# The top of layer 0 in a four-layer kernel: weights of layer 2 in four transfers, transpositions between the first products, small folds by row products

## The chip, the core and the metric

The kernel runs on one core of a Trainium2 chip. Everything is computed in fp32. The metric is device time in microseconds (us) from the first to the last instruction of one execution; the time of a kernel is the median of its runs.

The engines run side by side, each with its own instruction stream: TensorE (PE: products, and PEld: the loading of their stationary operand), VectorE (DVE), ScalarE (ACT), GpSimd (POOL) and SyncE (SP), which here only issues transfers. ScalarE and GpSimd issue transfers too. "ACTq" or "SPq" in a profile is the issue of a transfer on that engine's stream, "L776" is line 776 of the kernel.

## The reference

Four layers follow each other on an input x of 2 x 512 x 32 x 32. The change touches the top of layer 0, where two unrelated things are computed: the first steps of layer 0's attention, and products of weights that layer 2 needs much later. Layer 0, cut to what is spoken of here:

```python
xn = _bn(x, bn1_g, bn1_b)
q = _gconv1x1(xn, qw)                       # 8 groups of 64 channels
qg = q.reshape(b * GROUPS, DH, H, W)
off = conv(qg, off_dw_w, stride 4, 6 x 6, per channel)      # 36 taps
off = gelu(off + off_dw_b)
off = tanh(einsum('bchw,oc->bohw', off, off_pw_w)) * OFF_SCALE
...
pos = grid_q[:, :, None, :] - grid_kv[:, None, :, :]
bias = sign(pos) * log1p(abs(pos))
bias = relu(bias @ cpb_w1 + cpb_b1)
bias = relu(bias @ cpb_w2 + cpb_b2)
bias = (bias @ cpb_w3 + cpb_b3)
sim = einsum('bhid,bhjd->bhij', qh, kh) + bias
...
```

Layer 2:

```python
qkv = einsum('oc,bchw->bohw', w_qkv, xn) + b_qkv
attn = softmax(einsum('bci,bcj->bij', q, k) * scale)
out = einsum('bcj,bij->bci', v, attn)
proj = einsum('oc,bchw->bohw', w_proj, out) + b_proj
```

Its weights can be multiplied with each other ahead of time: Wq with Wk, and Wv with W_proj (the two "folds", 512 x 512 each), and the biases likewise (two vectors of 512: Wk times the bias of q, and W_proj times the bias of v, plus b_proj).

## The kernel before

`layer0` begins with loads and a stretch of preparation, and then runs a loop over `i` (256 iterations) that makes layer 0's attention bias: in each iteration VectorE forms four table sums (`first`, L599: 128 x 1024 sums of two short tables), TensorE multiplies them by `cpb_w2` in four parts (`second`, L616, tile z: 32 output partitions for each of four points, so that four products stand in different quarters of the partitions), ScalarE applies the relu (L625), and VectorE joins two parts (`joined`, L630). `first` runs up to 7 sums ahead of the products. Its results stand in a ring of eleven tiles: three of their own, then six pieces of the tile that holds layer 2's `qkv2` weights, and two of `proj2`'s; so a sum can be written there only when these weights are no longer read, and the sum number 11 needs the tile of number 0, which all four parts of the first iteration read.

The order on every engine is fixed: `in_order` makes each instruction follow the one before it in the program's text on the same engine. What one engine waits for thus holds up all that stands behind it on that engine. Pieces of work are written as generators, and calls of `advance` and `drain` lay out by hand how they interleave:

- `offsets(t)`: the query product pq (L389), its copy with bias `qb` to `qpad` by ScalarE (L391), 36 taps (for t = 0 on VectorE, L423 and L425), Gelu, the small product po (L441), tanh (`th`), a change of ScalarE's function table, sign, abs and log (`sgn`, `pos`), and the store of the tables `slog_d`. `load_tabs` and `scale_tab` bring them back for `first`.
- `bias_weights`: sorts and turns `cpb_w2`: prow, below, pcount, pw2t, pparts, pw2, and many small VectorE operations on the tile `few`.
- `key_weights`: transposes the block-diagonal `qw` and `kw` (twq, L789, with ScalarE's copies qwn and kwn, L791) and multiplies them (pkw, L797; copy kq_w, L798). Its result is first used in the loop.
- `transposed(j, k)`: the four 128 x 128 transpositions of chunk k of Wq, Wk or Wv (tile tw, L776) and two ScalarE copies of 128 x 256 to `nat` (tile bridge, L778), twelve times.
- `fold`: eight products over four chunks (tile pf, L135), every second one followed by a ScalarE copy of 128 x 1024 (`folded`, L835) and a store. The folds 4 to 7 read `proj2` in place.
- `small_fold`: the bias of q spread over the partitions by four products with the identity (row, L843), four products and sums with it on VectorE (`t2_b`, L849 and L850), and, in four steps, four products of one column each with `proj2` (pb, by `accumulate`, L135), then `o2_b` on VectorE (L855).

Products and transpositions write to three rotating PSUM tiles (`zt`); the tile `sim` is a fourth. The pool `h2q` has three buffers, which take the relu results of parts 1 and 3 in the loop and short-lived rows before it.

The loads: SP issues the constants, `qw`, `kw` (two transfers each, L229), `cpb_w2`, `vb2` and chunks 1 to 3 of x[0] (L242); ScalarE issues chunk 0 of x[0] (L218), then `qkv2_w` in four transfers and `proj2_w` in four (`load_w`, L119). GpSimd first clears `qw`, `kw` and `vw` whole (L224). `late_loads` (x[1] and `vw`) and the loop's tables follow on SP. In the loop the generators `small_steps` (what is left of it), `offsets(1)` and `samples(0)` are chained as `behind`, two steps for each iteration.

Of the kernel before, what the change touches and what calls it, by code (L numbers as in the profile page):

```python
# [19 lines left out]
P = 128  # L20
B, C, H, W = 2, 512, 32, 32
HW = H * W
CC = C // P
# [56 lines left out]
def kernel(ctx: ExitStack, tc: tile.TileContext, a: dict, out: bass.AP):  # L80
# [111 lines left out]
    def layer0(l0, fold_d, t2_b, o2_b):  # L192
# [26 lines left out]
        qkv2, proj2 = load_w(wa, "wa", [a["qkv2_w"], a["proj2_w"]], nc.scalar)  # L219
# [3 lines left out]
        for w in bd.values():  # L223
            nc.gpsimd.memset(w, 0.0)  # L224
# [7 lines left out]
        load_groups("kw")  # L232
# [9 lines left out]
        nc.sync.dma_start(out=xs[0][:, 1:, :], in_=a["x"][0, P:, :].rearrange("(k p) n -> p k n", p=P))  # L242
# [16 lines left out]
        pqb = zt([P, NPAIR], "pqb")  # L259
        for pr in range(NPAIR):  # L260
            nc.tensor.matmul(pqb[:, pr : pr + 1], bd["qw"][:, pr, :], col("bn1_b", pr), start=True, stop=True)
        nc.vector.tensor_copy(qb, pqb)
# [509 lines left out]
        def transposed(j, k):  # L772
# [4 lines left out]
            for i in range(2):  # L777
                nc.scalar.copy(nat[j][i][:, :, k * P : (k + 1) * P], tw[:, 2 * i : 2 * i + 2, :])  # L778
# [20 lines left out]

        steps = offsets(0)  # L800
        advance(steps, 2)
        bias_steps = bias_weights()
        next(bias_steps)
        key_steps = key_weights()
        advance(key_steps)
        advance(steps, 4)
        advance(bias_steps)
        advance(steps, 20)
        drain(key_steps)
# [6 lines left out]
        nat = [[next(h2p).rearrange("p (k n) -> p k n", k=2) for _ in range(2)] for _ in range(3)]  # L816
        wq, wk, wv = [lambda o, n, w=w: w[o // 2][:, o % 2, n] for w in nat]
        everything = slice(0, C)
        pb2 = ps_s.tile([P, CC], F32, name="pb2", tag="sim")
# [19 lines left out]
        def small_fold():  # L839

            row = zt([P, C], "row")
            for o in range(CC):
                nc.tensor.matmul(  # L843
                    row[:, o * P : (o + 1) * P], col("qkv2_b", o).to_broadcast([P, P]), ident, start=True, stop=True
                )
            yield
# [4 lines left out]
            for m in range(CC):  # L851
                n = slice(m * P, (m + 1) * P)
                accumulate(pb2[:, m : m + 1], [(proj2[:, o, n], vb2[:, o : o + 1]) for o in range(CC)])
                yield
            nc.vector.tensor_tensor(o2_b, pb2, col("proj2_b", 0, CC), ALU.add)  # L855

        fold_steps, small_steps = fold(), small_fold()
        for k in range(CC):
# [8 lines left out]
        advance(small_steps)  # L867
        advance(fold_steps)
        advance(small_steps)
# [3 lines left out]
        for _ in range(5):  # L873
            advance(fold_steps)
            advance(small_steps)
        drain(fold_steps)

# [1388 lines left out]
```

## Time and profile before

| | |
|---|---|
| median of 3 runs | 3350.77 us (3349.29 to 3352.3) |
| the profiled execution: its own time | 3353.46 us |
| the profiled execution: span | 3351.7 us, mean granted TensorE clock 0.998 |
| VectorE, ScalarE, GpSimd busy | 80%, 54%, 20% of the span |
| first product of the loop (z, L616) | 59.64 us |
| HBM read, written | 71.46 MB, 10.83 MB |

A profile shows one execution. Busy time is counted for each engine; the chain of waits goes back from the last instruction, at each step to what released it, and names its pieces with start and length; the timeline lists the instructions of an engine with, in brackets, the idle time before them and what ended it. The page divides the span into 40 slices of 84 us, so the whole preparation lies in the first one.

### The profile page before, as it was taken

The page shows a single profiled execution, that of the slowest core. Times are in us where ns is not written, and L with a number is a line of the kernel's source. Part 1 is how long each engine was busy: PE and PEld are TensorE (multiplying, and loading weights), DVE is VectorE, ACT ScalarE, POOL GpSimd, SP SyncE. Part 2 cuts the span into 40 slices and gives each one's busy share as a digit, 9 for nine tenths or more (in the row PEclk, how much of TensorE's full clock was granted, in tenths as well). Part 3 has the DMA queues.
Part 4 walks back from the last instruction along what each step waited for, and adds up shares of the span by engine and source line. Part 5 has one row for each costly group of instructions (what it writes and reads, how often), then busy time and mean ns, then how long its engine had stood idle before and what let it go on. Part 6 is the DMA issues. An engine that isn't in the chain of part 4 may idle for free.

```text
span 3351.7 us, 61808 instructions
## 1 busy us (share of the span) xinstructions
PE 3323.8 (99%) x24813; PEld 1611.7 (48%) x24813; DVE 2673.0 (80%) x3540; ACT 1805.5 (54%) x2774; POOL 676.7 (20%) x804
## 2 busy tenths in 40 slices
PE   9999999999999999999999999999999999999999
PEld 4333333332333332333333339999953443687777
DVE  6999999999999799999999976455446465665556
ACT  4866877877877577877877652122136245122221
POOL 0333333333333233333333310000000000000000
PEclk9999999999999999999999999999999999999999
DMA  5778787787787577787787751000100000000111
GB/s 166 157 161 166 153 168 156 152 166 153 158 167 155 103 162 155 159 169 152 158 166 157 161 135 58 14 8 14 52 0 14 26 29 20 7 7 3 30 32 36
DMA packets 142488, 343.97 MB, mean 103 GB/s; under 512 B 36464, under 2 KB 51440, under 8 KB 141424
## 3 DMA queue, kind: packets, MB, share of 16 engines
q0 software_dynamic: 68400, 231.26, 36.5%
q1 hardware_dynamic: 72496, 103.95, 10.7%
q8 instruction: 197, 3.23, 0.4%
q10 hardware_dynamic: 1296, 4.72, 0.4%
q14 instruction: 99, 0.81, 0.1%
HBM read 71.46 MB, written 10.83 MB: 25 GB/s over the span
## 4 chain that ended last, share of the span: by engine, by line
PE 82%; DVE 9%; issue 5%; DMA 2%; ACT 1%; POOL 1%; DVEq 0%; SPq 0%; POOLq 0%; ACTq 0%
PE z L616 38%; PE pma L135 6%; PE pw L1435 6%; PE pmb L135 5%; PE pmv L1435 4%; PE score L1614 3%; PE pv L1626 3%; DVE wa L599 3%; PE pm L1435 3%; PE score L1435 3%; PE pmt L1435 1%; PE ppr L1435 1%; DVE h L599 1%; DMA bridge<-h 1%; DVE bridge L630 1%
## 5 line engine op out<-in xcount | busy, mean ns | idle before, releaser
L616 PE MATMUL z<-wa,cpb_w 128*32 128x512 f32 x11904 | 1779.2, 593 | 5.8 <-ACT h L625 3.7
L625 ACT ACTIVATE h<-z,b2h 128x1024 f32<-128x1024 f32 x768 | 851.3, 1114 | 347.9 <-PE z L616 310.6
L616 PE MATMUL z<-h,cpb_w 128*32 128x512 f32 x4480 | 983.2, 593 | 1.6 <-ACT h L625 1.6
L616 PEld LDWEIGHTS z<-wa,cpb_w 128*32 128x32 f32 x11904 | 497.2, 110 | 888.2 <-issue 778.1
L599 DVE CUSTOM_DVE_ANT_1 wa<-tab,tab 128x1024 f32<-128x1024 f32 x744 | 878.1, 1216 | 1.3 <-PE z L616 1.1
L616 PEld LDWEIGHTS z<-h,cpb_w 128*32 128x32 f32 x4480 | 256.6, 110 | 328.6 <-issue 292.1
L599 DVE CUSTOM_DVE_ANT_1 h<-tab,tab 128x1024 f32<-128x1024 f32 x280 | 332.9, 1216 | 2.3 <-PE z L616 2.2
L630 DVE SCALAR_TENSOR_TENSOR h<-h,turn,h 128x1024 f32<-128x1024 f32 x256 | 326.8, 1276 | 4.3 <-ACT h L625 4.3
L625 ACT ACTIVATE bridge<-z,b2h 128x1024 f32<-128x1024 f32 x162 | 180.8, 1116 | 121.4 <-PE z L616 119.0
L927 POOL DMA_DIRECT2D bridge<-bridge x150 | 127.6, 850 | 547.2 <-DMA bridge<-h 510.5
L630 DVE SCALAR_TENSOR_TENSOR bridge<-bridge,turn,h 128x1024 f32<-128x1024 f32 x162 | 206.8, 1277 | 4.2 <-ACT bridge L625 4.2
L934 POOL DMA_DIRECT2D bridge<-h x161 | 163.4, 1015 | 213.2 <-DVE h L630 123.6
L1278 ACT COPY p<-pma 128x128 f32<-128x128 f32 x80 | 21.3, 266 | 334.7 <-PE pma L135 334.7
L1270 DVE TENSOR_TENSOR upper<-pma,p 128x256 f32<-128x256 f32 x80 | 33.7, 422 | 178.6 <-ACT p L1278 178.5
L1615 ACT ACTIVATE p<-score 128x512 f32<-128x512 f32 x256 | 130.0, 624 | 81.2 <-PE score L1614 79.6
L927 POOL DMA_DIRECT2D h2j<-h2j x90 | 76.2, 847 | 323.0 <-DMA h2j<-h 293.6
L1647 DVE TENSOR_TENSOR acc<-acc,p 128x1024 f32<-128x1024 f32 x96 | 111.0, 1217 | 19.4 <-ACT p L1615 19.3
L625 ACT ACTIVATE h2j<-z,b2h 128x1024 f32<-128x1024 f32 x94 | 105.0, 1117 | 37.9 <-PE z L616 37.3
L1614 PE MATMUL score<-q,k 64*128 64x512 f32 x512 | 120.7, 604 | 1.1 <-DVE gm L1191 1.1
L630 DVE SCALAR_TENSOR_TENSOR h2j<-h2j,turn,h 128x1024 f32<-128x1024 f32 x94 | 120.0, 1276 | 0.0
L1626 PE MATMUL pv<-p,vT 128*64 128x512 f32 x512 | 116.5, 598 | 0.0
L937 POOL DMA_DIRECT2D bridge<-h2j x90 | 111.9, 1244 | 2.6 <-issue 1.8
(458 smaller groups left out, 4379.8 us busy)
## 6 DMA issues: line engine op xcount, KB each, us to landing
bridge<-h POOLq DMA_DIRECT2D x161, 512.0 KB, 5.5
h2j<-h POOLq DMA_DIRECT2D x94, 512.0 KB, 5.9
bridge<-bridge POOLq DMA_DIRECT2D x159, 256.0 KB, 3.9
tab<-slog_d SPq DMA_DIRECT2D x128, 256.0 KB, 4.6
h2j<-h2j POOLq DMA_DIRECT2D x90, 256.0 KB, 3.2
bridge<-bridge POOLq DMA_DIRECT2D x150, 128.0 KB, 5.4
bridge<-bridge SPq DMA_DIRECT2D x90, 128.0 KB, 3.7
bridge<-h2j SPq DMA_DIRECT2D x90, 128.0 KB, 3.6
```

The lines of the kernel that those rows point to most:

```text
L135: nc.tensor.matmul(pm, w, m, start=(k == 0), stop=(k == len(pairs) - 1))
L599: nc.vector._custom_dve(TENSOR_ADD_SAT, out=h1.rearrange("p (y x) -> p y x", x=W), in0=tx[:, point, :].unsqueeze(1).to_broadcast([P, H, W] ...
L616: nc.tensor.matmul(z[point * 32 : point * 32 + 32, n], cpb_w2[:, lo : lo + 32], h1s[point][:, n], start=True, stop=True,)
L625: nc.scalar.activation(h2, z, AF.Relu, bias=b2h[:, part : part + 1])
L630: nc.vector.scalar_tensor_tensor(h2, h2, turn[:, part // 2 : part // 2 + 1], parts.pop(part + 1), ALU.mult, ALU.add)
L927: nc.gpsimd.dma_start(out=own[0:P:2], in_=own[1:P:2], accum_op=ALU.add)
L934: nc.gpsimd.dma_start(out=joins[i - 1], in_=other, accum_op=ALU.add)
L937: nc.gpsimd.dma_start(out=joins[i - 3 - j][j:P:4], in_=joins.pop(i - 3)[2:P:4], accum_op=ALU.add)
L1435: nc.tensor.matmul(out, stationary(l, k), moving(r, k), start=start and k == 0, stop=k == nk - 1, skip_group_check=not start,)
L1614: nc.tensor.matmul(sc, ks[m][r, s * P : (s + 1) * P], qs[m][r, n], start=True, stop=True)
L1615: nc.scalar.activation(p[:, part], sc, AF.Exp, scale=64 ** -0.5)
L1626: nc.tensor.matmul(pv[half][part * 64 : part * 64 + 64], vt[s % 4][:, lo : lo + 64], lps[s, half][:, part, :], start=(s == 0), stop=(s == 7),)
```

## The change

- Loads on ScalarE's queue: chunk 0 of `qkv2_w`, chunk 1, then chunks 2 and 3 in one transfer; `proj2_w` in one transfer, and behind it chunks 1 to 3 of x[0] (from SP's queue), both placed in the text behind the first two steps of `offsets(0)`, that is behind the copy to `qpad`.
- GpSimd clears only the halves of `qw`, `kw` and `vw` that no transfer writes (six instructions instead of three).
- On SP: `qw`, `cpb_w2`, `vb2`, then the bias of q as 512 numbers into a DRAM row `row_d`, `kw`, and that row back to all partitions (`row`, 128 x 512). The four row products on TensorE are gone.
- `qb`: the first column is made before pq, the other three behind the transpositions of chunk 0; the PSUM tile is the one of `sim`.
- `nat` is one view for each j, and `transposed` makes one copy of 128 x 512 in place of two of 128 x 256.
- Order: `transposed(j, 0)` stands directly behind the query product, `transposed(j, 1)` behind the second step of `bias_weights`, and chunks 2 and 3 where all four were. `key_weights`, which ran in two pieces around the first taps, runs in one piece behind `drain(steps)`, between the folds 1 and 2.
- `small_fold`: the products with `t2_b` in four steps; then four products of one 128 x 32 operand (a bias column repeated) with a row of `proj2`, 512 wide and permuted (steps of 128 elements), each into a quarter of the partitions; a ScalarE copy to `o_row`; four transfers on SP that spread one row each over the partitions (`few`, 128 x 4); four steps later four small VectorE additions. The transfers and the additions now run in the loop, ahead of `offsets(1)`.

```diff
-        qkv2, proj2 = load_w(wa, "wa", [a["qkv2_w"], a["proj2_w"]], nc.scalar)
+        w_2 = wa.tile([P, 4 * HID], F32, name="wa", tag="wa")
+        qkv2 = w_2[:, : CC * 3 * C].rearrange("p (k n) -> p k n", n=3 * C)
+        proj2 = w_2[:, CC * 3 * C :].rearrange("p (k n) -> p k n", n=C)
+
+        def load_rows(w, name, lo, hi):
+            nc.scalar.dma_start(
+                out=w[:, lo:hi, :], in_=a[name][lo * P : hi * P, :].rearrange("(k p) n -> p k n", p=P)
+            )
+
+        load_rows(qkv2, "qkv2_w", 0, 1)
...
-        for w in bd.values():
-            nc.gpsimd.memset(w, 0.0)
+        for h in range(2):
+            r, other = [slice(k * DH, (k + 1) * DH) for k in (h, 1 - h)]
+            for w in bd.values():
+                nc.gpsimd.memset(w[r, :, other], 0.0)
...
         load_groups("qw")
-        load_groups("kw")
+        load_rows(qkv2, "qkv2_w", 1, 2)
+        load_rows(qkv2, "qkv2_w", 2, 4)
...
-        nc.sync.dma_start(out=xs[0][:, 1:, :], in_=a["x"][0, P:, :].rearrange("(k p) n -> p k n", p=P))
+        row_d = dram.tile([CC, P], F32, name="row_d")
+        row = h2q.tile([P, C], F32, name="row", tag="h2")
+        lo = _PC_AT["qkv2_b"][0]
...
+            nc.sync.dma_start(out=row_d.rearrange("o p -> p o"), in_=a["pc"][:, lo : lo + CC])
+        load_groups("kw")
+        nc.sync.dma_start(out=row, in_=row_d.rearrange("o p -> (o p)").partition_broadcast(P))
...
-        pqb = zt([P, NPAIR], "pqb")
-        for pr in range(NPAIR):
+        pqb = ps_s.tile([P, NPAIR], F32, name="pqb", tag="sim")
+
+        def query_bias(pr):
             nc.tensor.matmul(pqb[:, pr : pr + 1], bd["qw"][:, pr, :], col("bn1_b", pr), start=True, stop=True)
-        nc.vector.tensor_copy(qb, pqb)
+
+        query_bias(0)
+        nc.vector.tensor_copy(qb[:, :1], pqb[:, :1])
...
-            for i in range(2):
-                nc.scalar.copy(nat[j][i][:, :, k * P : (k + 1) * P], tw[:, 2 * i : 2 * i + 2, :])
+            nc.scalar.copy(nat[j][:, :, k * P : (k + 1) * P], tw)
...
         steps = offsets(0)
         advance(steps, 2)
+        load_rows(proj2, "proj2_w", 0, 4)
+        nc.scalar.dma_start(out=xs[0][:, 1:, :], in_=a["x"][0, P:, :].rearrange("(k p) n -> p k n", p=P))
+        for j in range(3):
+            transposed(j, 0)
+        for pr in range(1, NPAIR):
+            query_bias(pr)
+        nc.vector.tensor_copy(qb[:, 1:], pqb[:, 1:])
         bias_steps = bias_weights()
         next(bias_steps)
         key_steps = key_weights()
-        advance(key_steps)
         advance(steps, 4)
         advance(bias_steps)
+        for j in range(3):
+            transposed(j, 1)
         advance(steps, 20)
-        drain(key_steps)
...
-            row = zt([P, C], "row")
-            for o in range(CC):
-                nc.tensor.matmul(
-                    row[:, o * P : (o + 1) * P], col("qkv2_b", o).to_broadcast([P, P]), ident, start=True, stop=True
-                )
-            yield
             for k in range(CC):
                 product = h2q.tile([P, C], F32, name="product", tag="h2")
                 nc.vector.tensor_tensor(product, qkv2[:, k, C : 2 * C], row, ALU.mult)
                 nc.vector.tensor_reduce(t2_b[:, k : k + 1], product, AX.X, ALU.add)
-            for m in range(CC):
-                n = slice(m * P, (m + 1) * P)
-                accumulate(pb2[:, m : m + 1], [(proj2[:, o, n], vb2[:, o : o + 1]) for o in range(CC)])
                 yield
-            nc.vector.tensor_tensor(o2_b, pb2, col("proj2_b", 0, CC), ALU.add)
+            pb = zt([P, C], "pb")
+            for k in range(CC):
+                nc.tensor.matmul(
+                    pb[32 * k : 32 * k + 32],
+                    vb2[:, k : k + 1].to_broadcast([P, 32]),
+                    proj2[:, k, :].rearrange("p (m q) -> p q m", m=CC),
+                    start=True,
+                    stop=True,
+                )
+            o_row = h2q.tile([P, C], F32, name="o_row", tag="h2")
+            nc.scalar.copy(o_row, pb)
+            yield
+            few = one.tile([P, CC, CC], F32, name="o_few")
+            with nc.allow_non_contiguous_dma("2048 numbers"):
+                for k in range(CC):
+                    nc.sync.dma_start(
+                        out=few[:, k], in_=o_row[32 * k : 32 * k + 1].rearrange("o (q m) -> o q m", m=CC)
+                    )
+            for _ in range(4):
+                yield
+            nc.vector.tensor_tensor(o2_b, few[:, 0], col("proj2_b", 0, CC), ALU.add)
+            for k in range(1, CC):
+                nc.vector.tensor_add(o2_b, o2_b, few[:, k])
...
-        for k in range(CC):
+        for k in range(2, CC):
             for j in range(3):
                 transposed(j, k)
...
         drain(steps)
-        advance(small_steps)
+        drain(key_steps)
         advance(fold_steps)
-        advance(small_steps)
+        advance(small_steps, CC)
         load_tabs(0)
         for ax in range(2):
             scale_tab(0, ax)
-        for _ in range(5):
-            advance(fold_steps)
-            advance(small_steps)
+        advance(fold_steps, 3)
+        advance(small_steps)
         drain(fold_steps)
```

More of the change, by code (lines that the diff above doesn't have):

```diff
@@ L241, in layer0 @@
             nc.sync.dma_start(out=vb2, in_=a["vb"][1].rearrange("(k p) -> p k", p=P))
-        nc.sync.dma_start(out=xs[0][:, 1:, :], in_=a["x"][0, P:, :].rearrange("(k p) n -> p k n", p=P))
+        row_d = dram.tile([CC, P], F32, name="row_d")
+        row = h2q.tile([P, C], F32, name="row", tag="h2")
+        lo = _PC_AT["qkv2_b"][0]
+        with nc.allow_non_contiguous_dma("512 numbers"):
+            nc.sync.dma_start(out=row_d.rearrange("o p -> p o"), in_=a["pc"][:, lo : lo + CC])
+        load_groups("kw")
+        nc.sync.dma_start(out=row, in_=row_d.rearrange("o p -> (o p)").partition_broadcast(P))
         def late_loads():
@@ L798, in key_weights @@
             nc.scalar.copy(kq_w, pkw)
+        nat = [bridge[:, 2 * j : 2 * j + 2, :].rearrange("p h (k n) -> p (h k) n", k=2) for j in range(3)]
+        wq, wk, wv = [lambda o, n, w=w: w[:, o, n] for w in nat]
         steps = offsets(0)
         advance(steps, 2)
+        load_rows(proj2, "proj2_w", 0, 4)
[5 more added lines that the diff above has]
+        nc.vector.tensor_copy(qb[:, 1:], pqb[:, 1:])
         bias_steps = bias_weights()
@@ L812, in layer0 @@
         )
-        nat = [[next(h2p).rearrange("p (k n) -> p k n", k=2) for _ in range(2)] for _ in range(3)]
-        wq, wk, wv = [lambda o, n, w=w: w[o // 2][:, o % 2, n] for w in nat]
         everything = slice(0, C)
-        pb2 = ps_s.tile([P, CC], F32, name="pb2", tag="sim")
         folds = [
```

## The prediction

> **What bounds the kernel now.** I read the page first: TensorE is busy for nearly the whole span, and the chain of work that ended last lies on it.
>
> ```profile
> PE 3323.8 (99%) x24813; PEld 1611.7 (48%) x24813; DVE 2673.0 (80%) x3540; ACT 1805.5 (54%) x2774; POOL 676.7 (20%) x804
> ```
>
> The change lies ahead of the loop over `i`, whose first product z starts at 59.64 us. So I read the chain of waits from 9 to 62 us next (start, length, what):
>
> ```profile
> 9.86 1.84 PE pqb L261 x8
> 11.70 3.64 PE pq L389 x4
> ...
> 15.41 1.16 ACT qpad L391
> ...
> 18.19 1.13 PE pkw L797 x8
> ...
> 19.93 5.81 ACT bridge L778 x21
> ...
> 25.79 3.70 PE pf L135 x8
> ...
> 34.16 1.00 PE row L843 x8
> ...
> 35.20 3.70 PE pf L135 x8
> 38.90 0.79 PE pb L135 x8
> ...
> 52.66 6.97 PE pf L135 x16
> 59.64 2.69 PE z L616 x21
> ```
>
> TensorE, with ScalarE's copies L778 in the middle, sets when the loop begins; after 25.79 it hardly pauses. In the loop TensorE is busy for 60.00 of 60 us from 60 to 120 and 58.34 of 60 to 180 (busy time by stretch), and one wait stands in the groups by line, near 175 us, on VectorE (after the count: busy us, mean ns, idle before and what ended it):
>
> ```profile
> L616 PE MATMUL z<-wa,cpb_w 128*32 128x512 f32 x768 | 118.4, 593 | 1.6 <-DVE kvbd L534 1.6
> ```
>
> VectorE itself, in its timeline, idles once at the loop's start and then has no idle time up to that wait:
>
> ```profile
> 65.26 1.28 DVE L630 SCALAR_TENSOR_TENSOR bridge<-bridge,turn,h 128x1024 f32<-128x1024 f32 x1
> 68.71 2.36 DVE L599 CUSTOM_DVE_ANT_1 h<-tab,tab 128x1024 f32<-128x1024 f32 x2 [2.17 <-PE z L616]
> ```
>
> So the result is the shift of the loop's first z, plus what the wait near 175 us becomes.
>
> **Start.** The `qw` transfers go out at 1.66 us and land 7.3 to 7.8 us later; nothing ahead of them changes, so pqb still starts at 9.86. Six of its eight passes (0.213 us apart) go behind pq, which then starts when qws is ready (9.85 + 0.28 us on VectorE), at 10.3 in place of 11.56; qpad moves from 15.41 to 14.15: -1.25. GpSimd's six half memsets stay off this path.
>
> **Transfers.** The next weight transfer of ScalarE's queue is issued at 9.74 now, 7.4 us after the first, and SP's own waits put 3.7 us ahead of the issue of x down to `in_qw`, which the code doesn't ask for; I assume chunks 1 to 3 are held as long again. 2.3 MB at the 401 to 423 GB/s seen from 12.1 to 22.3 us take 5.7 us: about 18 us, where the transpositions of chunk 2 are due at 20. The split by use therefore hides nothing that was exposed: chunk 0 landed by 9.2 (1.86 + 7.3), and its first transposition ran at 19.1 because of TensorE's order. Moving x and proj2 behind qpad on ScalarE's queue costs two issues of 0.45 us, under qpad's 1.15; SP loses its issue of x (0.38). Behind them on ScalarE wait the copies of chunk 0, and behind those TensorE: if one of the issues must wait there for the landing of an earlier transfer as x does now, up to 3 us. On SP `kw` and the broadcast row follow `row_d`; they are used only after 31 us.
>
> **Transpositions between the first products.** Chunk 0's twelve run at half clock from 13.9 to about 16.1, the six pqb passes (0.11 each at full clock) to 16.8. Now the VectorE copy of qb[:, 1:] waits for these, the small `few` operations are queued behind it and prow behind them (17.3), then below, pcount, pw2t: chunk 1's transpositions start at 18.7. The 24 taps on VectorE are queued behind the same wait: they start at 18.1 in place of 16.59 and end at 29.4; po needs them only after fold 1 (31.7), which covers it with 1.6 us after the Gelu; gone, it would cost the excess. Nine groups of four transpositions remain. Now 24 copies of 128x256 come every 0.277 us (6.65/24), 0.55 a group; a copy of 128x512 takes 0.60 by itself (qwn), between 0.52 and 0.60 in a row. At 0.53 the first fold starts at 23.6 (24.2 at 0.60) in place of 25.79: **-2.2** (-1.6).
>
> **Key weights behind fold 1.** Their old place cost little: it is in the step above. The new one stands behind `drain(steps)`, so ScalarE must first do this, by its timeline:
>
> ```profile
> 34.13 1.01 ACT L835 COPY folded<-pf 128x1024 f32<-128x1024 f32 x1 [2.53 <-PE pf L135]
> ...
> 35.24 1.28 ACT L375 ACT_TABLE_LOAD   x1
> ...
> 37.20 0.26 ACT L468 ACTIVATE pos<-pos 128x64 f32<-128x64 f32 x1
> ```
>
> Fold 1 ended at 33.88, pos at 37.46: 3.58 later. Only then come the copies qwn and kwn (0.55 + 0.60), then pkw (1.0 to the next product), and fold 2 is queued behind pkw: 5.75 us after fold 1, where it is 1.32 now (po, row 1.00, the wait for folded). That is **+4.4**, with TensorE idle for some 2.8 us of it. The row matmuls' 1.00 us is inside this difference. If this cover of old (row) were kept and the stall hidden, it would be 0; I see no work in TensorE's order that could hide it.
>
> **Small folds.** Four pb groups go: 4 x 0.79 = 3.16. In their place 8 passes of 128x32 by 512. They write four different quarters of the partitions, as z's do, and 32 of z's take 3.57 us in the chain's next piece: 0.9 for 8. One by one, as pf's 8 in 3.44, they take 3.4. That the moving operand steps over 512 bytes no row shows. The nearest is z: 0.95, so **-2.2** (upper end +0.3).
>
> The Trainium skill, SBUF — State Buffer, section Door 1: The DMA port swizzle, says that reads which change the 16-byte line each time pay a penalty; no row here shows it, and at twice the time for the 8 passes the sum would be 0.9 us more, my estimate.
>
> Sum for the first z: -2.2 + 4.4 - 2.2 = 0.0.
>
> **The clock.** In the granted clock by stretch (PE busy first; PEclk is the first number after POOL):
>
> ```profile
> 5.27:8.68 3.41, 1.32 (x3) 0.26 (x2) 0.00 (x0) 0.00 (x0) 0.00 (x0) 1.00 1.07 268
> 8.68:12.10 3.42, 2.24 (x9) 2.21 (x10) 0.65 (x5) 0.00 (x0) 0.00 (x0) 0.50 0.39 85
> 12.10:15.51 3.41, 3.41 (x6) 1.41 (x5) 0.74 (x8) 0.10 (x1) 0.00 (x0) 0.50 1.02 423
> 22.34:25.75 3.41, 3.28 (x24) 2.37 (x23) 3.41 (x15) 3.41 (x15) 0.00 (x0) 1.00 0.40 145
> ```
>
> A stretch with 1.32 of 3.41 us busy was followed by half clock, one of 3.41 by full. Fold 1 to fold 2 leaves TensorE busy for about 1.4 of its first 4.75 us, so the clock can fall there; that costs 0, or 1.3 to 3.0 us (one stretch: the 2.6 us of work left in it take twice as long; the next one whole adds 3.41/2). The fall after the first row came 2.1 us after the last warm-up product (6.59), so a pause of 2.8 us is enough: I take **+1.3**. The last row holds transpositions alone but for its start and end, at full clock; I let them count as work where the clock must rise, in 12.10 to 15.51.
>
> The same skill, TensorE: Matmul & The Clock Gate, section HAM oscillation, allows gaps up to some 3.4 us: by it the total would be 1.3 us less, and the first row contradicts it. Its Part 4: PE-mode transpose says that transpositions do not raise the clock: by it the case of cold transpositions below would be the forecast, and the last row shows only that they do not lower it.
>
> **In the loop.** The second half of `small_fold` goes ahead of `offsets(1)`: pq (1.91) leaves the first iteration and VectorE's next table sum at 68.71 comes 1.9 earlier after the loop's start; four additions with their waits (0.16 each, 0.2 apart) take 0.75 back. TensorE gains nothing by the deferral; the 1.6 us wait near 175 shrinks by 1.9 - 0.75 (bounds 0 and 1.6): **-1.2**. The four transfers of `few` (2048 numbers) stand on SP behind x[1] (2 MB, 11.9 us to landing): x[1] is issued 4.05 us after the first z, so `few` lands about 16.5 after it (4.05 + 11.9 + 0.5). VectorE reaches the additions at 17.6 (9.07 - 1.91 + six table sums of 1.135 + three joins of 1.2): hidden by a margin of 1.1; later, it costs the excess, with every table sum behind it. Their four issues (0.4 us each) hold nothing up on SP, whose next transfer is due at 76.9.
>
> **Sum.** 0.0 + 1.3 - 1.2 = +0.1. The profiled execution took 3353.46 (span 3351.7), 0.08% over the median 3350.77; the difference is put on the median: **3351.0**. Ends: all terms good (0 for the clock, -1.6) -1.6; all bad (fold start +0.6, pb +2.5, clock +1.7, wait 0 instead of -1.2) +6.
>
> **Rivals.** *The stall is hidden* (no idle before fold 2): -4.4 - 1.2 = 3345.2. For it, TensorE has its own queue; against it, the fixed order and ScalarE's timeline. Chance 0.10. *Buffers (slower)*: `o_row` holds one of three h2q buffers, which part 1 and 3 of each iteration write in turn, until `few` lands. If the third of these (five z parts of 1.72, 8.6 us after the loop's start) gets it, ScalarE waits to 16.5: +8, 3359; it decides if that buffer is given out ahead of part 1's, which VectorE releases at about 6.0 (two z, an activation, a join). For it, an order fixed at build; against it, that earlier release. 0.09. *Cold transpositions*: the clock rises only with the folds: nine groups at 0.88 (twice four spacings of 0.11) for 0.53, and one stretch of folds at half, 1.7: +4.9, 3356; against it the last stretch shown. 0.07. *The split puts chunk 1 ahead of qw's landing*: +2 to 3 on everything, 3353.5. For it, nothing in the code but the order; against it the hold until 9.74. 0.07. What is left, 0.67, is my forecast: the shifts cancel, its own range 3348 to 3354.
>
> **Chances.** 0.2% is 6.7 us, about what a measurement of this kernel can tell from no change. Half of the first rival with the good end of the clock and the wait passes it: faster 0.06. Buffers, and a part of cold transpositions with a bad end: slower 0.13. Same 0.81. Range 3345.5 to 3358: it takes the first rival's edge and most of the second.
>
> **What would show it.** First pq at 10.3; first pf near 23.6; a pause of TensorE between twq and pkw near 33 to 36 with ScalarE in Ln; fold 2 5.75 after fold 1; first z at 59 to 61; no h activation waiting on a transfer from o_row. I am wrong if first z moves by over 4 us or the loop shows a new wait.

## The result and the profile after

The changed kernel took 3360.57 us (median of 9 runs, 3355.56 to 3362.87), the kernel before 3350.57 beside it (9 runs, 3348.89 to 3352.3): ratio 1.0027, 95% interval 1.0017 to 1.0037. It is 10 us slower; forecast were 3351.0 and a range of 3345.5 to 3358. The profiled execution took 3360.91, its span is 3359.1 (before: 3351.7). The page shows that no work was added (PE after the change; busy us, share, instructions):

```profile
PE 3325.5 (99%) x24781; PEld 1612.0 (48%) x24781; DVE 2674.5 (80%) x3544; ACT 1804.7 (54%) x2763; POOL 675.6 (20%) x807
```

The loss is ahead of the loop. The chain of waits of the changed kernel (start, length, what):

```profile
1.65 6.04 DMA bridge<-in_qw
...
7.71 5.20 DMA bridge<-in_kw
...
12.93 0.56 PE pqb L281 x2
13.49 3.62 PE pq L411 x4
...
22.76 3.64 PE tw L798 x16
...
28.53 3.70 PE pf L135 x8
...
36.82 1.01 ACT folded L862
...
37.92 1.28 ACT L397
...
40.61 0.49 ACT kwn L812
...
41.15 2.08 PE pkw L818 x8
43.23 15.51 PE pf L135 x32
58.74 2.16 PE pb L875 x7
...
67.96 7.41 PE z L638 x65
```

The first z stands at 67.96 where it was 59.64: +8.3. The first two pieces are one wait: pqb waits for the second half of `qw`, which lands at 12.79 (the semaphores of the trace; the chain names the `kw` transfer on the same tile). 13 of its 16 parts are there by 8.49, the last three at 10.90, 12.69 and 12.79. From the first z to the last, 0.7 us come back (the shift is +8.33 at the first z and +7.62 at the last), so the span grows by 7.4.

The granted clock by stretch in the changed kernel (stretch, length, busy us of PE, PEld, DVE, ACT and POOL with counts, PEclk, DMA share, GB/s):

```profile
19.38:22.79 3.41, 2.44 (x20) 1.99 (x18) 2.22 (x14) 1.29 (x5) 0.00 (x0) 1.00 1.00 374
22.79:26.21 3.42, 3.42 (x16) 3.42 (x17) 3.06 (x15) 2.33 (x4) 0.00 (x0) 0.50 1.04 413
26.21:29.62 3.41, 3.09 (x21) 2.26 (x20) 3.41 (x16) 2.54 (x5) 0.00 (x0) 1.00 0.45 174
...
36.45:39.86 3.41, 1.60 (x11) 0.95 (x9) 1.22 (x9) 2.98 (x6) 0.00 (x0) 1.00 0.34 143
39.86:43.27 3.41, 2.12 (x9) 2.12 (x10) 3.03 (x6) 1.22 (x4) 0.00 (x0) 0.50 0.12 31
43.27:46.69 3.42, 3.42 (x5) 1.35 (x5) 2.88 (x5) 0.58 (x1) 0.00 (x0) 0.50 0.63 143
```

After the start, where it is at half from 9.14 to 19.38 us (8.68 to 15.51 before), the clock falls twice: behind the waits for `sort` (2.44 of 3.41 us busy), so that 16 transpositions run at 0.213 us each instead of 0.109; and behind the stall of the key weights (1.60 busy), for two stretches.

### The profile page after: what moved, and what is told of

It reads as the page before. It is cut to its first block, busy times and chain, and to the rows that moved or that the text cites. A ratio compares the mean times of both kernels' runs of the same rounds, so it can differ in the third digit from the quotient of the medians.

```text
span 3359.1 us, 61727 instructions
## 1 busy us (share of the span) xinstructions
PE 3325.5 (99%) x24781; PEld 1612.0 (48%) x24781; DVE 2674.5 (80%) x3544; ACT 1804.7 (54%) x2763; POOL 675.6 (20%) x807
## 4 chain that ended last, share of the span: by engine, by line
PE 88%; DVE 6%; issue 3%; DMA 2%; ACT 1%; POOL 0%; DVEq 0%; SPq 0%; ACTq 0%; POOLq 0%
PE z L638 45%; PE pma L135 6%; PE pw L1468 6%; PE pmb L135 5%; PE pmv L1468 4%; PE score L1647 3%; PE pv L1659 3%; PE pm L1468 3%; PE score L1468 3%; DVE wa L621 2%; PE ppr L1468 1%; PE pmt L1468 1%; PE sim L667 1%; PE pp L727 1%; PE pf L135 1%
## 5 line engine op out<-in xcount | busy, mean ns | idle before, releaser
L960 POOL DMA_DIRECT2D bridge<-bridge x150 | 127.5, 850 | 539.2 <-DMA bridge<-h 494.9
L970 POOL DMA_DIRECT2D bridge<-bridge x90 | 110.8, 1231 | 1.7 <-DMA bridge<-bridge 1.1
```

Of the source, the lines that this page charges most:

```text
L960: nc.gpsimd.dma_start(out=own[0:P:2], in_=own[1:P:2], accum_op=ALU.add)
```

## The experiments

All stand against the changed kernel's median 3360.6; the kernel before took 3350.3 to 3351.3 beside them. "Landed" is the second half of `qw`, "packets" counts the weight packets of 6144 bytes among the first 30 us that took over 1 us (median 0.23), both from the trace of the profiled execution.

| run | median us | ratio to before (95%) | landed | packets | first fold | first z |
|---|---|---|---|---|---|---|
| before | 3350.57 | 1 | 9.72 | 0 | 25.79 | 59.64 |
| the change | 3360.57 | 1.0027 (1.0017 to 1.0037) | 12.79 | 36 | 28.53 | 67.96 |
| h1_hold_chunks | 3359.56 | 1.0025 (1.0016 to 1.0034) | 11.13 | 32 | 28.35 | 66.71 |
| h2_row_one_packet | 3359.65 | 1.0023 (1.0014 to 1.0033) | 11.24 | 6 | 26.27 | 64.70 |
| h4_no_four_byte | 3357.39 | 1.0023 (1.0014 to 1.0032) | 9.65 | 2 | 23.04 | 61.48 |
| h5_row_late | 3356.76 | 1.0018 (1.0009 to 1.0027) | 10.25 | 6 | 25.45 | 64.86 |
| h6_x_later | 3358.24 | 1.0023 (1.0014 to 1.0032) | 13.01 | 30 | 29.49 | 67.71 |
| h7_keys_first | 3363.65 | 1.0037 (1.0023 to 1.0051) | 8.94 | 57 | 30.12 | 68.11 |
| h3_small_late | 3352.90 | 1.0013 (1.0004 to 1.0022) | 8.49 | 5 | 20.33 | 58.83 |
| k1_keys_between_folds | 3354.04 | 1.0012 (1.0003 to 1.0021) | 8.52 | 31 | 24.72 | 58.33 |
| p1_pb_rows_in_order | 3357.53 | 1.0019 (1.0010 to 1.0029) | 11.86 | 29 | 27.39 | 65.62 |
| c2_keys_and_rows | 3352.51 | 1.0006 (0.9997 to 1.0015) | 11.71 | 34 | 26.89 | 59.42 |
| c3_keys_rows_small_late | 3348.07 | 0.9994 (0.9985 to 1.0003) | 8.63 | 4 | 22.93 | 55.45 |
| c5_bias_columns_later | 3348.20 | 0.9992 (0.9983 to 1.0001) | 10.38 | 5 | 23.41 | 55.94 |
| c6_chunk1_early | 3348.13 | 0.9990 (0.9981 to 0.9999) | 9.04 | 5 | 21.10 | 53.63 |

One profile stands for one execution; landings differ between executions, so the medians decide and the traces say where. The changed kernel's own nine runs lie 7.3 us apart and the intervals of the ratios reach 3 us and more to either side: a difference of less than some 3 us between two medians is not shown by the times alone.

### The first transfers

On SP the changed kernel issues the small pieces ahead of `kw` (its timeline; start, length):

```profile
1.65 1.42 SPq L240 DMA_DIRECT2D bridge<-in_qw  x2
3.11 0.60 SPq L246 DMA_DIRECT2D cpb_w<-in_cpb_w  x1
3.76 0.65 SPq L253 DMA_DIRECT2D vb<-in_vb  x1
4.45 0.61 SPq L259 DMA_DIRECT2D row_d<-in_pc  x1
5.11 3.19 SPq L240 DMA_DIRECT2D bridge<-in_kw  x2
```

**Chunk 1 held back.** It was sent at 5.57, not at 9.74 as before, and I suspected a collision with `qw`.

```diff
+        gate = one.tile([P, 2], F32, name="gate")
+        nc.scalar.copy(gate, bd["qw"][:, 0, DH - 1 : DH + 1])
         load_rows(qkv2, "qkv2_w", 1, 2)
         load_rows(qkv2, "qkv2_w", 2, 4)
```

> The changed kernel with one thing more: a ScalarE copy of two numbers per partition of the query weights stands ahead of the issue of the weight chunks 1 to 3, so these go out only when both halves of the query weights have landed. In the changed kernel the chunk 1 goes out at 5.57 us, the second half of the query weights lands at 12.79 and the first pqb runs at 12.93 (9.86 before). Theory (collision: chunk 1 delays the query weights): pqb back at 9.8 to 10.2, the first fold about 3 us earlier than 28.53 (25.0 to 26.0), the first z at 64.5 to 65.5 instead of 67.96, the time 3 us under the changed kernel's 3360.6, about 3357.5. Rival (the 512 four-byte writes of the bias row, which SP issues at 4.45, delay them): pqb stays at 12.5 to 13.2 and the time at 3360.

3359.56: one us of the three, and within the runs' spread. `qw` still lands at 11.13 with nothing of chunk 1 beside it, so chunk 1 is not what makes it late; and the held chunks 2 and 3 now land at 23.18, for which the transpositions wait (tw at 23.32). The rival named the bias row:

```diff
-            nc.sync.dma_start(out=row_d.rearrange("o p -> p o"), in_=a["pc"][:, lo : lo + CC])
+            nc.sync.dma_start(out=row_d.rearrange("o p -> (o p)"), in_=a["vb"][1])
```

> The changed kernel, but the bias row in DRAM is filled by a transfer of contiguous rows (16 pieces of 128 bytes, the value bias in place of the query bias), not by 512 four-byte writes; so the small output vector t2_b is made from another bias. Every other transfer goes out as in the changed kernel. Theory (chunk 1 collides with the query weights): pqb stays at 12 to 13.2 and the time within 1 us of 3360.6. Rival (the four-byte writes delay the query weights): pqb at 9.8 to 10.3, first z near 65, time about 3357.5. If both share it, pqb lies between, near 11.

`qw` at 11.24, between the two. The slow weight packets go from 36 to 6 and the first z comes 3.3 us earlier, but the median falls by 0.9 only: in this profile the way from the first z to the end of the span took 2.8 us longer (3294.0 against 3291.2), as it can between executions of one kernel (section on the base). What the four-byte writes cost in this order is thus not shown by the times.

**Old order, no small pieces, one piece late.** The old order of all first transfers with the bias row late; then the new order without four-byte pieces:

```diff
         load_groups("qw")
+        load_groups("kw")
...
-        load_groups("kw")
-        nc.sync.dma_start(out=row, in_=row_d.rearrange("o p -> (o p)").partition_broadcast(P))
...
         advance(bias_steps)
+        row_cols = one.tile([P, CC], F32, name="row_cols")
+        nc.vector.tensor_copy(row_cols, col("qkv2_b", 0, CC))
+        with nc.allow_non_contiguous_dma("512 numbers"):
+            nc.sync.dma_start(out=row_d.rearrange("o p -> p o"), in_=row_cols)
+        nc.sync.dma_start(out=row, in_=row_d.rearrange("o p -> (o p)").partition_broadcast(P))
```

> The changed kernel with the order of the first transfers as before the change: on SP both halves of the query weights, then those of the key weights, then the 64 KB of cpb_w2 and the value bias; the bias row goes to DRAM only later, from a copy of four columns that VectorE makes behind pcount (about 22 us), and back to all partitions. Seen so far: in the runs of the changed kernel and its variants the second half of the query weights landed at 12.79, 11.13, 11.24, 8.52 and 11.86 us, on 3, 6, 4, 0 and 6 of the 16 DMA engines late, and about as many packets of 6144 bytes of weight chunk 0 took 1 to 2 us between 4.8 and 6.2 us where 0.23 is their usual time. Theory (what SP issues from 3.1 to 5.1 us, the 1024 four-byte pieces above all, holds the engines up): no such packet over 1 us, landing at 8.0 to 9.8, first z 2 to 4 us earlier (64 to 66), median 3357 to 3358. Rival (the rest of the change, that is GpSimd's half clears or chance alone): landing again at 10.5 to 13 on some engines and median 3359.5 to 3360.6.

```diff
-        with nc.allow_non_contiguous_dma("512 numbers"):
-            nc.sync.dma_start(out=vb2, in_=a["vb"][1].rearrange("(k p) -> p k", p=P))
+        nc.sync.dma_start(out=vb2, in_=a["vb"][1].rearrange("(p k) -> p k", k=CC))
...
-            nc.sync.dma_start(out=row_d.rearrange("o p -> p o"), in_=a["pc"][:, lo : lo + CC])
+            nc.sync.dma_start(out=row_d.rearrange("o p -> (o p)"), in_=a["vb"][1])
```

> The changed kernel with its order of transfers, but the two small vectors are loaded without four-byte pieces: the bias row as 16 pieces of 128 bytes (from the value bias) and the value bias as 128 pieces of 16 bytes, so its columns hold other elements; both small output vectors differ from the reference by that. Theory (four-byte pieces hold the engines up): no 6144-byte packet over 1 us between 4.8 and 6.2 us, query weights landed by 9.8, median 3357 to 3358 as in the run with the old order. Rival (the order itself: the wait of the key weights for the landing of earlier transfers, and chunk 1 sent at 5.57 us): landing at 10.5 to 13, median 3359 to 3360.6.

The old order gives 7.7 us back (3352.90), more than any theory had said: `qw` lands at 8.49, and the first fold runs at 20.33, since in this execution TensorE starts before its clock has fallen (full from 6.72 to 34.03 us). Luck has a part in that: in c3_keys_rows_small_late below, which is the same up to fold 1, `qw` lands at 8.63, the clock is at half from 9.80 to 13.21 and from 16.63 to 20.04, and the first fold runs at 22.93. And four of the eleven runs of h3_small_late took 3356.7 to 3358.4, the other seven 3351.0 to 3353.2; by means, 3354.2 against 3359.5, the old order gives 5.3. Without four-byte pieces but in the new order it is 3.2. Two runs ask which part of the order counts: the bias row alone late (`kw` left where it was), and x issued behind the copies of chunk 1.

```diff
-            nc.sync.dma_start(out=row_d.rearrange("o p -> p o"), in_=a["pc"][:, lo : lo + CC])
         load_groups("kw")
-        nc.sync.dma_start(out=row, in_=row_d.rearrange("o p -> (o p)").partition_broadcast(P))
...
+            nc.sync.dma_start(out=row_d.rearrange("o p -> p o"), in_=row_cols)
+        nc.sync.dma_start(out=row, in_=row_d.rearrange("o p -> (o p)").partition_broadcast(P))
```

> The changed kernel with one thing less among the first transfers: the bias row goes to DRAM and back only later (from four columns that VectorE copies behind pcount). The order of the query weights, cpb_w2, value bias and key weights stays that of the changed kernel. By this chunk 1 of the weights waits for the first half of the query weights, and the transfer of x on ScalarE's queue no longer waits for the landing of the bias row (14.4 to 16.0 us in the runs seen). Theory (the bias row does most of the harm, once by its 512 four-byte writes and once by the wait of x's issue, with the copies of chunk 0 behind it): query weights landed by 10.5, fold 0 at 20 to 24 us, median 3353 to 3355.5, near the 3352.9 with all of the old order. Rival (the place of the key weights and of the value bias does it): median 3357 to 3360.

```diff
-        nc.scalar.dma_start(out=xs[0][:, 1:, :], in_=a["x"][0, P:, :].rearrange("(k p) n -> p k n", p=P))
         for j in range(3):
             transposed(j, 0)
...
         for j in range(3):
             transposed(j, 1)
+        nc.scalar.dma_start(out=xs[0][:, 1:, :], in_=a["x"][0, P:, :].rearrange("(k p) n -> p k n", p=P))
```

> The changed kernel, but ScalarE issues x behind the copies of chunk 1 instead of behind qpad; all transfers up to proj2 go out as in the changed kernel. In a run of a variant where the query weights landed early (8.52 us) that issue waited until 14.99 us for the landing of the bias row and held the copies of chunk 0 up by 3.2 us; where they landed late (12.8) it waited for nothing. Theory (the wait of x's issue binds only in the executions in which the query weights land early): median 0 to 1.5 us under the changed kernel, 3359 to 3360.6, the fastest execution 2 to 3 us under the fastest of the changed kernel's (3355.6). Rival (this wait is the main loss): median 3355 to 3357.

3356.76 lies between the bounds of theory and rival: by the medians the row is half of it (3.8 of 7.7). 3358.24 lies just below what the theory allows. Its 2.3 are within the runs' spread, so what x's wait costs in the time is not shown; it is not the main loss. Where `qw` happens to land early, it is seen on ScalarE (timeline of the run with the key weights moved, which has the changed kernel's transfers):

```profile
14.99 0.39 ACTq L826 DMA_DIRECT2D x<-in_x  x1
15.41 1.56 ACT L799 COPY bridge<-tw 128x512 f32<-128x512 f32 x3 [3.20 <-DMA row_d<-in_pc]
```

x asks for nothing of `row_d`; its issue waits for that landing because the transfers count their completions on eight counters in turn, and in this trace these two have the same one. The last run moves the one line of `kw` back and leaves the four-byte writes among the first transfers:

```diff
         load_groups("qw")
+        load_groups("kw")
...
             nc.sync.dma_start(out=row_d.rearrange("o p -> p o"), in_=a["pc"][:, lo : lo + CC])
-        load_groups("kw")
```

> The changed kernel with one line moved: the key weights' transfers stand directly behind those of the query weights again, ahead of cpb_w2 and the value bias; the bias row still goes to DRAM among the first transfers, with its 512 four-byte writes. The transfers count their completions on eight counters in turn, and one line more or less ahead changes which earlier landing each waits for: by this place chunk 1 waits for the second half of the query weights, the bias row for the first half, and x on ScalarE's queue no longer for the bias row. Theory (the place of the key weights, by what the others wait for, is the main loss): query weights landed by 10.5 in the profiled execution, x's issue without a wait, median 3352.5 to 3355. Rival (the four-byte writes themselves, early or a little later, hold the engines up): median 3356 to 3359.

The rival wins, and by more than it said: 3363.65 (5 runs), no better than the change, though `qw` lands at 8.94 and x waits for nothing. It differs from h3_small_late in the place of the row alone, and their medians are 10.8 us apart. The row goes out at 8.70 beside chunks 1 to 3. Stretches of this kernel, then of the one with the row late (columns as above, the last one GB/s):

```profile
10.00:15.00 5.00, 3.94 (x24) 2.69 (x22) 0.97 (x9) 2.71 (x4) 0.00 (x0) 1.00 1.11 110
15.00:20.00 5.00, 0.74 (x5) 0.58 (x5) 4.61 (x24) 0.64 (x2) 0.00 (x0) 0.83 0.63 58
```

```profile
10.00:15.00 5.00, 3.63 (x25) 2.65 (x23) 1.17 (x10) 2.85 (x5) 0.00 (x0) 1.00 0.99 401
15.00:20.00 5.00, 4.98 (x41) 4.18 (x41) 4.62 (x24) 4.21 (x10) 0.00 (x0) 1.00 1.03 401
```

And the issue of chunks 2 and 3 in the same two kernels (KB, median us from issue to landing):

```profile
wa<-in_qkv_w ACTq DMA_DIRECT2D x1, 1536.0 KB, 17.4
```

```profile
wa<-in_qkv_w ACTq DMA_DIRECT2D x1, 1536.0 KB, 7.7
```

With 2 KB in four-byte writes among them, the core's transfers move 58 to 110 GB/s instead of 401 and the same load takes 9.7 us longer to land; TensorE, at the transpositions of chunk 1, has 0.74 us of work in 5. In the changed kernel the same stretch (10 to 15 us) shows 103 GB/s. The column of packets says the same over all runs: 29 to 57 slow weight packets where these writes run among the weights, 0 to 6 where they don't. The Trainium skill, DMA: Bandwidth & Descriptors, section Specifications, gives 512 bytes as the least for full rate and says that smaller transfers are read, changed and written. No run here shows the reading back; what they show is the slower packets of the transfers beside it.

### The stall of the key weights

```diff
         drain(steps)
-        drain(key_steps)
         advance(fold_steps)
...
-        advance(fold_steps, 3)
+        advance(fold_steps)
+        advance(key_steps)
+        advance(fold_steps)
+        drain(key_steps)
+        advance(fold_steps)
```

> The changed kernel with the key weights moved again: the transpositions twq behind fold 4, the product pkw behind fold 5, so that ScalarE's copies between them run under a fold. Theory (stall behind fold 1 and the clock that falls with it): TensorE's pause of 2.6 us at 38.5 goes, the clock stays at full from 26.2 us on, fold 2 starts 0.2 to 0.6 us after fold 1 instead of 6.44, twq and pkw cost 0.9 us each at full clock; from the end of fold 1 to the first z 25 to 26 us instead of 31.17: first z at 62 to 63, time about 3354.8. Rival (what is gained there is lost at the loop's start, because the first table sums or the ring tiles become the wait): first z at 62 to 63 too, but the loop's later z products shifted by the old +7 to +8, time 3358 to 3361.

3354.04, 6.5 us less, as the theory said; the first z comes at 58.33, ahead of its 62 to 63, because `qw` landed at 8.52 in this profile. TensorE's timeline of this run (counted from 0, twq stands behind fold 3 and pkw behind fold 4):

```profile
32.95 7.11 PE L135 MATMUL pf<-bridge 128*128 128x512 f32 x16
39.90 1.04 PE L810 MATMUL twq<-cst,bridge 128*128 128x128 f32 x8
41.16 3.70 PE L135 MATMUL pf<-wa,bridge 128*128 128x512 f32 x8 [0.23 <-ACT folded L862]
44.70 1.05 PE L818 MATMUL pkw<-qwn,kwn 128*128 128x128 f32 x8
```

Fold 2 follows fold 1 at once, the copies of twq run under fold 4, and pkw takes 1.05 at full clock. From the end of fold 1 (32.98) to the first z it is 25.35 us, against 31.17.

### The products with the bias

```diff
-                    proj2[:, k, :].rearrange("p (m q) -> p q m", m=CC),
+                    proj2[:, k, :],
...
-            nc.scalar.copy(o_row, pb)
+            nc.scalar.copy(o_row.rearrange("p (q m) -> p q m", m=CC), pb.rearrange("p (m q) -> p q m", m=CC))
```

> The changed kernel, but the four bias products read the rows of proj2 in order (steps of 4 bytes instead of 512), and ScalarE's copy to o_row does the permutation. Theory (the stride of the moving operand costs the time): the eight pb passes take 0.9 to 1.0 us instead of 2.16 (each 0.59 as z's, not 1.05), first z 1.2 us earlier, 66.7, time about 3359.4. Rival (the small columns-repeated operand or four writers of one tile cost it): pb stays at 2.0 to 2.2 and the time at 3360.6. ScalarE's permuted copy may take up to twice its 0.58 us; nothing waits for it before the transfers at 73.7.

Tile pb in the changed kernel, then in this one (least, median and greatest ns of one):

```profile
L875 PE MATMUL pb<-wa,vb x8: 1047/1081/1309, 58.7 to 59.8; 128*32 128x512 f32 x8
```

```profile
L875 PE MATMUL pb<-wa,vb x8: 592/604/617, 57.5 to 58.0; 128*32 128x512 f32 x8
```

The stride is the cost: 2.16 us for the eight become 1.00. ScalarE's permuted copy takes 0.586, as long as the plain one. The median falls by 3.0, more than the 1.2 that the trace explains; the rest is within the runs' spread, and `qw` landed 0.9 earlier in this profile.

### Together

The edits of the two sections above in one kernel, and then the old order of transfers with them:

> The changed kernel with two edits that helped one by one: the key weights between the folds 4 to 6, and the bias products reading the rows of proj2 in order. Theory (they add up): from the end of fold 1 to the first z 24.2 us (25.35 less 1.07); median about 3354.0 - 1.2 to 3.0, that is 3351 to 3353. Rival (the ring of table sums or the tables are the next wait): no gain over 3354.0 with the key weights alone.

> The three edits together: key weights between folds, bias products in order of rows, first transfers in the old order with the bias row late. Theory (the transfers' order costs 2 to 4 us in most executions): first pqb at 8.3 to 10, first z at 55.5 to 57.5, median 2 to 4 us under the run with the first two alone, 3347.5 to 3350, which is under the 3351.2 of the kernel before. Rival (the late engines are chance and come in both orders alike): median equal to that run within 1 us.

3352.51 and 3348.07: the two edits of TensorE add up within the runs' spread, and the order of transfers is worth another 4.4. The edits behind them fill TensorE's waits for `sort`: the late columns of `qb` behind prow, then chunk 1's transpositions too.

```diff
-        for pr in range(1, NPAIR):
-            query_bias(pr)
-        nc.vector.tensor_copy(qb[:, 1:], pqb[:, 1:])
         bias_steps = bias_weights()
         next(bias_steps)
+        for pr in range(1, NPAIR):
+            query_bias(pr)
+        nc.vector.tensor_copy(qb[:, 1:], pqb[:, 1:])
```

> The kernel with the three edits together (key weights between folds, bias products in order of rows, old order of transfers), and the three late columns of the query bias behind the product prow instead of ahead of it, so that they fill TensorE's wait for the sort of cpb_w2. Theory: TensorE's pauses between 14.7 and 17 us shrink by about 0.9 us, the stretch there stays busy enough for the clock to stay at full (it fell from 16.6 to 20.0 us in the run without this): first z at 52.8 to 54.6 instead of 55.45, median 3345.5 to 3347.5. Rival (VectorE's copy of these columns now comes behind the sort and delays pcount by as much): first z at 55 to 56, median 3348.

```diff
         nc.vector.tensor_copy(qb[:, 1:], pqb[:, 1:])
+        for j in range(3):
+            transposed(j, 1)
...
         advance(bias_steps)
-        for j in range(3):
-            transposed(j, 1)
```

> The same as the run sent with it, and the transpositions of weight chunk 1 also ahead of pcount, directly behind the late query bias columns. Theory (they fill the waits for the sort): another 0.5 to 1 us less, first z at 52 to 54, median 3345 to 3347. Rival (chunk 1, issued near 8.3 us, lands only at 12 to 12.5 and the transpositions now wait for it, or VectorE's taps start later and become the wait at po): no gain, or 0.5 us more than the run sent with it.

3348.20 and 3348.13, short of their forecasts by 0.7 and 1.1: the rivals' numbers (3348, and no gain), and no gain over 3348.07 is shown. In the first, `qw` landed 1.75 later than in the run before, so its first z of 55.94 tells nothing on the edit; the clock did not fall again after it had risen at 16.98. In the second the first z comes at 53.63, with the clock at full from 12.45 on. The last kernel's interval, 0.9981 to 0.9999, lies below the kernel before, and it takes 12.4 us less than the change. Its chain:

```profile
21.10 3.70 PE pf L135 x8
...
41.24 0.89 PE pkw L811 x8
42.13 3.44 PE pf L135 x8
45.57 1.00 PE pb L875 x8
46.56 7.06 PE pf L135 x16
53.63 17.30 PE z L631 x160
```

### The base

The kernel before, unchanged, profiled twice more:

> The kernel before, profiled once more. In its first profile the query weights landed at 9.72 us, one engine late, the first pqb ran at 9.86, the first z at 59.64, and that execution took 3353.46, 2.7 over the median of the runs shown. Theory (that execution was one with a late landing, and the median stands for an earlier one): here landing at 8.0 to 9.0 and first z at 57.0 to 59.0, if this execution lies near the median of 3350.7. Rival (the start is always as in the first profile and the difference arises in the loop): pqb at 9.7 to 9.9 and first z at 59.4 to 59.9 whatever the time.

> The same once more, so that three executions of the kernel before stand beside each other: time and first z should move together within 1 us by the theory; by the rival the first z stays at 59.4 to 59.9.

They took 3349.70 and 3347.33; `qw` landed at 8.71 and 8.74, the first z came at 58.44 and 58.45. So the first profile was 1.2 late at the first z. But these two differ by 2.4 us with the same first z: the theory that time and first z move together falls. Between the first and the last z the first profile lost another 2.2 to 3.9 on them; up to the 2000th z, at 286 us, the three run alike within 0.1, so these executions of one kernel drift apart later, and what makes them do so stays open. Measured from 58.45 the change moves the first z by 9.5, and 10.0 stand between the medians. The loop can't be placed against these: from the first z to the last, the changed kernel's profile is 0.7 shorter than the first of the three and 1.5 and 3.2 longer than the others.

## Why the prediction was wrong

Term by term, against the profiled execution of before (the change of each):

| stretch | forecast | measured |
|---|---|---|
| start to first pqb | 0 | +3.07 |
| pqb to the first fold | -2.19 | -0.33 |
| first fold to the end of fold 1 | 0 | +0.01 |
| end of fold 1 to fold 2 | +4.43 | +5.28 |
| fold 2 to first z (pb -2.2, clock +1.3) | -0.9 | +0.29 |
| loop, first z to last | -1.2 | -0.7 (0.0 up to 286 us) |

**The step that failed is the one on the transfers.** It said that nothing ahead of `qw` changes, that chunks 1 to 3 are held as long as before, and that `kw` and the broadcast row follow `row_d` and "are used only after 31 us". It asked when the row is needed, and not what its 512 four-byte writes do to the transfers beside them, nor which issue waits for its landing. The runs put 7.7 us of median on that order (5.3 by means; 4.4 with the two edits of TensorE in place): 3.8 go with the row alone, and the run with `kw` first, 10.8 above its pair with the row late, shows the mechanism, transfers at a seventh to a quarter of their rate while the weights load. How the other 3.9 divide between the place of `kw`, the value bias's four-byte reads and the early chunk 1 stays open. Why single DMA engines are late with `qw` was not seen in the trace; they are late with chunk 0 of `qkv2_w` too, which lands 0.2 to 0.6 us ahead of `qw` in all of these profiles but one. The rival "chunk 1 ahead of qw's landing" named the right place and sign and the size of the start's shift (+2 to 3), though not the time (3353.5), at 0.07; its cause is not the main one: holding chunk 1 gave 1.0.

**The step that I left as a bound, x waiting behind qpad for an earlier landing,** "up to 3 us", happened: 3.20 in one execution, hidden wherever `qw` was late.

**Transpositions.** The price of a group was right: nine groups take 4.57 us at full clock with the old order of transfers (0.51 each; forecast 0.53). What failed is the clock: I let it stay at full from 15.5, and the waits for `sort` left one stretch with 2.44 of 3.41 us busy, after which it fell. Four groups then took 3.64 us at half clock instead of 2.04: 1.6 of the 1.86 missing here. The late start is not needed for it: the clock fell at the same place in c3_keys_rows_small_late. My case of cold transpositions was half right, with another cause: transpositions alone raised the clock, after the stretch from 22.79 to 26.21. The Trainium skill, TensorE: Matmul & The Clock Gate, Part 4: PE-mode transpose, says that they don't count as busy in the same way; this row contradicts it.

**Key weights.** Right in place, reason and size. My 5.75 is counted from 33.88, where the small product behind fold 1 begins (the chain ends the fold itself at 34.04); from the same point it is 6.61 here (43.23 less 36.62), and 5.70 (34.11 less 28.41) in h3_small_late, whose pkw found the clock at full. TensorE idles 0.49 and 2.61 us, where I had 2.8. The clock's price was set too low: 0.9 in pkw and 1.4 in the folds behind it (15.51 against 14.13 with the key weights between the folds), 2.3 for 1.3, because the stretch with the stall is followed by two at half.

**Small folds.** The eight passes took 2.16, between my 0.95 and the bound of 3.4: -1.0, not -2.2. The choice of the nearest row was wrong, since z's operand doesn't step over 512 bytes. The rule of the Trainium skill, SBUF — State Buffer, section Door 1, a penalty for each access that crosses to a new 16-byte line, was the better guide; the runs show 2.2 times the time for these passes.

**The loop** gained nothing that is shown. As forecast, `few` held nothing up. VectorE's timeline shows the additions without idle time before them, 17.4 us after the first z (forecast 17.6):

```profile
84.20 1.28 DVE L652 SCALAR_TENSOR_TENSOR h<-h,turn,h 128x1024 f32<-128x1024 f32 x1
85.39 0.15 DVE L893 TENSOR_TENSOR o_b<-o_few,pc 128x4 f32<-128x4 f32 x1
85.58 0.56 DVE L895 TENSOR_TENSOR o_b<-o_b,o_few 128x4 f32<-128x4 f32 x3
```

So the rival with the buffers did not come. But the wait for kvbd fell by 0.4 only, from 1.63 to 1.22 us, and a new one of 0.5 for ScalarE's relu stands ahead of it (TensorE's waits from 60 to 300 us; us in total, times, longest):

```profile
PE z L638 <- DVE kvbd L556: 1.2, 1, 1.2
PE z L638 <- ACT h L647: 0.5, 1, 0.5
```

The 2000th z stands 225.99 us behind the first, before the change 226.01: of the 1.2 nothing came. The 0.7 at the last z arises later, where executions of the kernel before differ among themselves by up to 3.9.

**With the old order of transfers the time comes into the range**: median 3352.90, first z at 58.83 in the profile (forecast 60.9 with the clock). That is luck in part: there the clock stayed at full to 34.03, so pqb to the first fold took 4.2 less than before instead of 2.2, which pays for the small folds. The largest error is one edit that I costed at nothing, the order of the transfers; the small folds' 1.2, the loop's 1.2 and the 0.9 of a slow pkw stand beside it.

## What to carry to other kernels

A transfer whose data is needed late is not free because of that: price what its pieces do to the transfers beside it (512 four-byte writes cost a 1.5 MB load 9.7 us), and list which later issues wait for its landing, on every queue. Between two steps that need another engine's copies, lay work that needs nothing of it; the same key weights cost 6.5 us less two folds further on. A strided operand of a product is best tried against the permutation on the copy behind it, which cost nothing here.

## What the runs showed of the hardware

- The transfer of 512 four-byte numbers into DRAM took 13.7 us to land beside the weight load (h7_keys_first) and 9.9 beside proj2 and x (h3_small_late); single 6144-byte packets beside it took up to 4.9 us in h7_keys_first and 6.2 in k1_keys_between_folds (0.23 the median).
- Moving operand in steps of 512 bytes: four concurrent 128x32 products of 512 columns in 1.08 us each, 0.60 in order.
- The clock fell after stretches with 1.60 and 2.44 of 3.41 us busy, but not after one with 2.19 in the loop (196.87 to 200.28).
- Two executions of one kernel with the first z within 0.01 us of each other ended 2.5 us apart in span.
